# Moving product copies and normal-form evictions to ScalarE, and a bias load by one slot, in an encoder-decoder kernel

## The chip, the cores and the metric

The kernel runs on one core of a Trainium2 chip. Time is the device time of one execution in microseconds, the lower the better. Everything is in fp32. A core has TensorE (PE in the profile, with its weight loads as PEld), VectorE (DVE), ScalarE (ACT), GpSimd (POOL) and SyncE (SP), which here issues every DMA. Each engine has a queue of its own that runs in the order of the program; engines meet at semaphores.

## The reference

One layer of an encoder-decoder with batch 2, width 512, 16 heads of 32, a feed-forward width of 2048, 2048 target rows and 77 source rows. Cut to what matters:

```python
x = src                                    # (2, 77, 512)
x = x + _mha(_ln(x, n1), _ln(x, n1), enc_in, enc_out, enc_bias)
x = x + relu(_ln(x, n2) @ enc_ff1.T + b1) @ enc_ff2.T + b2
memory = x
y = tgt                                    # (2, 2048, 512)
yn = _ln(y, dec_n1)
y = y + _mha(yn, yn, dec_sa_in, dec_sa_out, self_bias + causal)
y = y + _mha(_ln(y, dec_n2), memory, dec_ca_in, dec_ca_out, cross_bias)
h = _ln(y, dec_n3)
y = y + relu(h @ dec_ff1.T + b1) @ dec_ff2.T + b2
```

`_ln` subtracts the mean, divides by the standard deviation, scales and adds. `_mha` projects to q, k and v, takes softmax(q k / sqrt(32) + bias) v for each head and projects out. The biases depend on the difference of positions alone.

## The kernel before

The 2 x 2048 target rows are eight blocks of 512 (two batches of four), each of four tiles of 128 tokens. The instruction order is written out by hand: the program text is the order on every engine.

The attention stage, up to about 1780 us of the span, makes causal self attention of all blocks, with the encoder and the cross attention of the first block (`first_cross`, 960 to 1250 us) in between. After it comes the feed-forward stage, which this change is mostly about. In it each block has 56 slots of feed-forward work, and one generator, `cross(x + 1)`, does the next block's cross attention beside it: before slot n of block x, the generator runs the functions that `plan[n]` holds. `cross(1)` runs ahead of the loop, partly beside the end of self attention; the last block has no companion. Only the fifth block (the first of the second batch) loads a bias in `cross`, for its tiles 0 and 1 (`biased`); those of the first block are loaded in `first_cross`.

The feed-forward matrices are multiplied with seven products instead of eight (`PARTS`): a slot forms one product of sums of quarters. Slots 0 to 27 are the first layer (seven products by four column groups n), slots 28 to 55 the second. `prepare(s + 3)` forms the operands of a slot three slots ahead: on GpSimd, and for the hidden rows of the second layer on VectorE (L1104). `first_product` writes one PSUM bank by eight matmuls (L1121). The bank is used for one or two quarters of the hidden rows `hT`; the first product that reaches a quarter copies into it (L1132, L1134, L1136), later ones add (L1138, VectorE), and after the last one ScalarE applies the relu (L1141). The banks 4 to 7 go round in turn. In the order (1, 4, 5, 7, 2, 3, 6) of all blocks but the first, L1134 runs in slots 0 to 11, once a slot: the second quarter of product 1, of product 4 and of product 5. In the first block's order (3, 5, 1, 4, 7, 2, 6) it runs in slots 0 to 3 and 12 to 15.

`norm_stages` makes a layer norm of a tile in three functions. `stats` has L718 to L720 on VectorE and a power on GpSimd (L721). `center` has L727 on VectorE, which writes the normalized tile into a ring of three buffers, and L728 on GpSimd, which adds a row to y in place. `turned` transposes four 128 x 128 pieces into one PSUM bank on TensorE (L733) and evicts each with scale and bias. In `cross`, the n2 norm of tile t has these in slots t, t + 2 and t + 4, and its results feed the q matmuls (`q_group`, L746) of slots 9 to 12; the n3 norm, which feeds the next block's feed-forward, has `turned` in slots 31, 38, 45 and 52. The y rows are loaded by L998, those of tiles 2 and 3 only after the results that lie in the same place have been stored (L1165) at the end of a block.

`attend_stages` of tile t stand in slots 14 + 7t and after: `score` (matmuls L760, then VectorE: with a bias L767, and L769, L770), `exp` (ScalarE, L773), `normalize` (L778, L779 on VectorE, L780 on GpSimd), `turned` (transposes L786, copies L788 and L790) six slots on, `times_v` (L797, the copy L801) and `out` (L806, L807). The probabilities lie in one buffer, `pr` (named oT in the profile), which the bias tile is loaded into (`bias_tile`, four DMAs, L103) before the scores are added.

Of the kernel before, what the change touches and what calls it, by code (L numbers as in the profile page):

```python
# [11 lines left out]
AF = mybir.ActivationFunctionType  # L12
ALU = mybir.AluOpType
# [4 lines left out]
P = 128  # L18
# [36 lines left out]
def tile_encoder_decoder(ctx: ExitStack, tc: tile.TileContext, ins, out):  # L55
    nc = tc.nc
# [20 lines left out]
    def vec(name, i):  # L77
        c = _COL[name] + i
        return vecs[:, c : c + 1]
# [16 lines left out]
    def bias_tile(dst, m, nq, nk, off):  # L96

        flat = tz[m].rearrange("h b t -> h (b t)")
        for r0 in range(0, nq, RB):
            n = min(RB, nq - r0)  # L100
            o = off - r0
            skew = flat[:, o : o + RB * (LT - 1)].rearrange("h (b u) -> b h u", u=LT - 1)
            nc.sync.dma_start(dst[r0 : r0 + n], skew[:n, :, :nk])  # L103
# [45 lines left out]
    with (  # L149
# [20 lines left out]
        def bank():  # L170

            i = count["bank"] % count["banks"]
            count["bank"] += 1
            return psum[:, i, :]
# [212 lines left out]
        got = {}  # L387
# [322 lines left out]
        def norm_stages(y, n, row, place, done):  # L710

            keep = {}

            def stats():
                st = sm.tile([P, 6], F32, name="bnst", tag="bnst")
                mv = sm.tile([P, 2], F32, name="cmv", tag="cmv", bufs=4)
                rs = sm.tile([P, 2], F32, name="crs", tag="crs", bufs=4)
                nc.vector.bn_stats(st, y())  # L718
                nc.vector.bn_aggr(mv, st)
                nc.vector.tensor_scalar_add(rs[:, 0:1], mv[:, 1:2], EPS)  # L720
                nc.gpsimd.tensor_tensor(rs[:, 1:2], rs[:, 0:1], mhalf[:, 0:1], ALU.pow)  # L721
                keep.update(mv=mv, rs=rs)

            def center():
                xn = keep["xn"] = place()
                mv, rs = keep["mv"], keep["rs"]
                nc.vector.tensor_scalar(xn, y(), mv[:, 0:1], rs[:, 1:2], ALU.subtract, ALU.mult)  # L727
                nc.gpsimd.tensor_tensor(y(), y(), row, ALU.add)  # L728

            def turned():  # L730
                xn, pt, dst = keep["xn"], bank(), done()
                for c in range(NC):
                    nc.tensor.transpose(pt[:, ts(c, P)], xn[:, ts(c, P)], ident)  # L733
                for c in range(NC):
                    sc, bi = vec(f"dec_{n}_s", c), vec(f"dec_{n}_b", c)
                    if c % 2:
                        nc.scalar.activation(dst[:, c, :], pt[:, ts(c, P)], AF.Identity, bias=bi, scale=sc)
                    else:
                        nc.vector.tensor_scalar(dst[:, c, :], pt[:, ts(c, P)], sc, bi, ALU.mult, ALU.add)

            return stats, center, turned

        def q_group(o, w, nT, dst):
            mm = bank()
            for c in range(NC):
                nc.tensor.matmul(mm, w[:, c, :], nT[:, c, :], start=(c == 0), stop=(c == NC - 1))  # L746
            nc.vector.tensor_scalar(dst, mm, vec("dec_ca_in_b", o), SCALE, ALU.add, ALU.mult)
# [140 lines left out]
        for x, (b, m) in enumerate(blocks):  # L888
# [14 lines left out]
            for t in range(TB):  # L903
                end = x == len(blocks) - 1
                jobs[u + NU + (2 if end else 7) + t].append(out_job(b, m, t))
                at = u + NU + ((-1, 0, 3, 4)[t] if end else 6 + t)
# [6 lines left out]
            for g in range(NC):  # L913
# [3 lines left out]
                at = u + g * TB - 3  # L917
# [74 lines left out]
        def y_of(x, t):  # L992
            return ys[x % 2][:, t, :]
# [27 lines left out]
        def late_loads():  # L1021
# [17 lines left out]
        PARTS = {  # L1039

            1: (((1, 1), "+", (2, 2)), ((1, 1), "+", (2, 2)), (("+", 1, 1), ("+", 2, 2))),
            2: (((2, 1), "+", (2, 2)), ((1, 1),), (("+", 2, 1), ("-", 2, 2))),
            3: (((1, 1),), ((1, 2), "-", (2, 2)), (("+", 1, 2), ("+", 2, 2))),
            4: (((2, 2),), ((2, 1), "-", (1, 1)), (("+", 1, 1), ("+", 2, 1))),
            5: (((1, 1), "+", (1, 2)), ((2, 2),), (("-", 1, 1), ("+", 1, 2))),
            6: (((2, 1), "-", (1, 1)), ((1, 1), "+", (1, 2)), (("+", 2, 2),)),
            7: (((1, 2), "-", (2, 2)), ((2, 1), "+", (2, 2)), (("+", 1, 1),)),
# [3 lines left out]
        def order_of(x, layer):  # L1051

            return ORDER[layer if x else 2]
# [20 lines left out]
        def in_ring(name, ring):  # L1074
            turns[name] += 1
            return ring[turns[name] % len(ring)]
# [38 lines left out]
        def first_product(s):  # L1115
            x, layer, i, n = slots[s]
            a, b = operands[s]
            mm = ff_bank()
            for f in range(2):
                for c in range(2):  # L1120
                    nc.tensor.matmul(  # L1121
                        mm[:, ts(f, TOK)], a[:, c, ts(f, P)], b[:, c, :], start=(c == 0), stop=(c == 1)
                    )
            order = order_of(x, 1)
            got = mm.rearrange("p (f n) -> p f n", f=2)
            for k, (sign, r, c) in enumerate(PARTS[i][2]):
                users = [j for j in order if (r, c) in [u[1:] for u in PARTS[j][2]]]
                f = (r - 1) * (NF // 2) + 2 * n
                dst = hT[:, f : f + 2, ts(c - 1, TOK)]
                if i == users[0]:  # L1130
                    if sign == "-":
                        nc.scalar.activation(dst, got, AF.Identity, scale=-1.0)  # L1132
                    elif k:
                        nc.vector.tensor_copy(dst, got)  # L1134
                    else:
                        nc.scalar.copy(dst, got)  # L1136
                else:
                    nc.vector.tensor_tensor(dst, dst, got, SIGN[sign])  # L1138
                if i == users[-1]:
                    for e in range(2):  # L1140
                        nc.scalar.activation(dst[:, e, :], dst[:, e, :], AF.Relu, bias=vec("dec_ff1_b", f + e))  # L1141
# [27 lines left out]
        def ff_bank():  # L1169
            count["mm"] += 1  # L1170
            return psum[:, 4 + count["mm"] % 4, :]
# [11 lines left out]
        def cross(x):  # L1183

            b, m = blocks[x]
            plan = [[] for _ in range(per)]

            def place(tag):
                if tag == "xr":
                    return lambda: sb.tile([P, D], F32, name=tag, tag=tag, bufs=2)  # L1190
                return lambda: in_ring("xt", xt_ring)

            def bias(t):
                bias_tile(pr.rearrange("p (h k) -> p h k", k=S), 2, P, S, 255 - P * t)

            for t in range(TB):
                fs = norm_stages(
                    lambda t=t: y_of(x, t), "n2", bv, place("xt"), lambda t=t: nT2[:, :, ts(t, P)]
                )
                for k, f in zip((0, 2, 4), fs):  # L1200
                    plan[t + k].append(f)
            for g in range(NC):
                plan[9 + g].append(lambda g=g: q_group(g, w_q[g], nT2, qT[g // 2][:, g % 2, :]))
            for t in range(TB):
                at = 14 + 7 * t
                y = lambda t=t: y_of(x, t)
                biased = m == 0 and t < 2
                if biased:
                    plan[at if t else at - 4].append(lambda t=t: bias(t))
                fs = attend_stages(  # L1210
                    lambda g, t=t: qT[g // 2][:, g % 2, ts(t, P)], kTcs[b], vcs[b], y, biased, pr,
                    lambda g: pts_all[:S, g, :], place("xr"), wbt,
                )
                for k, f in zip((0, 2, 3, 6, 9, 11), fs):
                    plan[at + k].append(f)
                fs = norm_stages(y, "n3", bo, place("xt"), lambda t=t: nTt[:, :, ts(t, P)])
                for k, f in zip((13, 15, 17), fs):
                    plan[at + k].append(f)
            for fs in plan:
                for f in fs:  # L1220
                    f()
                yield
# [6 lines left out]
        turned_to, scored_to, at = {n: 0 for n in range(end)}, {}, [0]  # L1229
# [18 lines left out]
        i = 0  # L1248
# [34 lines left out]
        nc.sync.dma_start(w_2, ins["dec_ff2_wT"].rearrange("(c p) o -> p c o", p=P))  # L1283
        count.update(bank=0, banks=4)
        side = cross(1)
        slot(end)
        for s in range(4):
# [12 lines left out]
        for x in range(len(blocks)):  # L1300
            if x:
                side = cross(x + 1) if x + 1 < len(blocks) else iter(())
            for n in range(per):
                if x or n >= 8:
                    next(side, None)
                    ff_slot(x * per + n)
# [37 lines left out]
```

## Time and profile before

| what | value |
|---|---|
| three runs | 2956.04, 2958.81, 2960.45 us (median 2958.81) |
| profiled execution | 2958.76 us, its span 2957.0 us |
| granted TensorE clock, mean over the span | 0.987 |
| L1134, copy on VectorE, 92 times | 684 ns (median) |
| L1136, copy on ScalarE, 32 times | 587 ns (median) |
| L739, eviction on VectorE, 128 times | 409 or 410 ns (medians) |
| L737, eviction on ScalarE, 128 times | 458 ns (median) |
| one block of the feed-forward stage with its companion | about 147 us |

The span is the time from the first to the last instruction on the engines; what lies around it is 1.8 us. In a line of the timeline stand the start, the duration, the engine, the line of the program, the operation, what it writes and reads, and in brackets how long the engine had been idle before and what ended that. In a list of waits stand who waited for whom, the total, the number of times and the longest. The profile puts a wait for several semaphores down to the one that came last.

### The profile page before, as it was taken

How to read it: one execution, taken by the hardware profiler on the slowest of the kernel's cores; microseconds unless marked ns; L12 is line 12 of the kernel's file. 1: busy time of each engine (PE TensorE's matmuls, PEld its weight loads, DVE VectorE, ACT ScalarE, POOL GpSimd, SP SyncE). 2: the span in 40 equal slices, each digit the busy share in tenths (PEclk: the TensorE clock that was granted, in tenths of full speed). 3: DMA queues.
4: the chain of work that ended last, by engine and by line, in shares of the span. 5: the costliest groups of instructions: out<-in, count | busy, mean ns of one | idle time of the engine just before them, and what ended most of it. 6: DMA issues, size and time to landing. Idle time of an engine off the chain costs nothing.

```text
span 2957.0 us, 60689 instructions
## 1 busy us (share of the span) xinstructions
PE 2875.8 (97%) x24440; PEld 2018.7 (68%) x24440; DVE 2202.4 (74%) x6171; ACT 1220.9 (41%) x2211; POOL 737.2 (25%) x601
## 2 busy tenths in 40 slices
PE   8899999999999999999999997999999999999999
PEld 5456666666666556666666675777777777777788
DVE  4767688888987788888878884767676777776765
ACT  3344456546665455555556671213131313131311
POOL 0100000000000101000000004464646464646464
PEclk9799999999999999999999999999999999999999
DMA  6313301201112502201101124000001000000000
GB/s 175 87 52 118 102 16 51 66 16 44 34 41 69 129 19 79 70 26 62 41 16 37 45 75 156 1 29 1 29 1 37 10 29 1 29 1 29 1 15 15
DMA packets 117643, 137.10 MB, mean 46 GB/s; under 512 B 18240, under 2 KB 73072, under 8 KB 117234
## 3 DMA queue, kind: packets, MB, share of 16 engines
q1 hardware_dynamic: 117362, 133.22, 15.5%
q8 instruction: 192, 3.15, 0.5%
q14 instruction: 89, 0.73, 0.1%
HBM read 111.33 MB, written 21.86 MB: 45 GB/s over the span
## 4 chain that ended last, share of the span: by engine, by line
PE 79%; DVE 13%; DMA 3%; issue 2%; POOL 2%; ACT 2%; SPq 0%; POOLq 0%; DVEq 0%; ACTq 0%
PE psum L1152 13%; PE psum L403 12%; PE psum L353 9%; PE psum L1121 8%; PE psum L420 7%; DVE pp L362 5%; PE psum L230 4%; PE psum L806 4%; PE psum L746 4%; PE psum L206 4%; PE psum L242 4%; PE psum L217 3%; DVE pp L369 3%; PE psum L786 2%; PE psum L797 1%
## 5 line engine op out<-in xcount | busy, mean ns | idle before, releaser
L379 ACT ACTIVATE pp<-pp,nm 128x128 f32<-128x128 f32 (+15 forms) x512 | 614.6, 1210 | 200.8 <-DVE nm L376 198.2
L362 DVE TENSOR_SCALAR_CACHE_REDUCE pp<-psum 128x512 f32<-128x512 f32 (+3 forms) x1024 | 558.3, 590 | 47.2 <-PE psum L353 45.3
L403 PE MATMUL psum<-ident,pp 128*128 128x128 f32 x4352 | 549.6, 279 | 18.3 <-DVE mx L369 11.8
L403 PEld LDWEIGHTS psum<-ident,pp 128*128 128x128 f32 x4352 | 475.1, 142 | 132.3 <-DVE pp L362 57.1
L409 ACT COPY pts<-psum 128x512 f32<-128x512 f32 (+3 forms) x592 | 299.1, 577 | 509.6 <-PE psum L403 400.6
L1104 POOL TENSOR_TENSOR vv<-pp 128x512 f32<-128x512 f32 x320 | 415.6, 1316 | 137.4 <-PE psum L1121 117.7
L407 DVE COPY pts<-psum 128x512 f32<-128x512 f32 (+2 forms) x544 | 329.9, 660 | 42.1 <-PE psum L403 39.3
L353 PE MATMUL psum<-kT,q 32*128 32x512 f32 (+3 forms) x2560 | 352.1, 579 | 4.6 <-ACT kT L222 1.6
L420 PEld LDWEIGHTS psum<-pts,vv 128*32 128x32 f32 x8704 | 226.2, 110 | 124.1 <-issue 116.9
L420 PE MATMUL psum<-pts,vv 128*32 128x128 f32 x8704 | 278.7, 275 | 0.2 <-DVE vv L233 0.2
L268 POOL TENSOR_TENSOR rstd<-rstd,mhalf 128x1 f32<-128x1 f32 x32 | 18.2, 570 | 929.8 <-DVE rstd L267 924.4
L1138 DVE TENSOR_TENSOR kT<-kT,psum 128x512 f32<-128x512 f32 x256 | 166.5, 680 | 98.3 <-PE psum L1121 80.5
L1141 ACT ACTIVATE kT<-kT,vecs 128x256 f32<-128x256 f32 x256 | 115.6, 502 | 299.8 <-DVE kT L1138 299.8
L369 DVE CUSTOM_DVE_ANT_0 pp<-psum,bias 128x256 f32<-128x256 f32 (+1 forms) x512 | 209.8, 410 | 20.9 <-PE psum L353 16.6
L353 PEld LDWEIGHTS psum<-kT,q 32*128 32x128 f32 x2560 | 119.4, 184 | 148.6 <-issue 99.4
L1152 PE MATMUL psum<-vv 128*128 128x256 f32 x768 | 176.9, 381 | 0.0
L1121 PE MATMUL psum<-oT,vv 128*128 128x256 f32 x736 | 166.5, 380 | 0.0
L1152 PEld LDWEIGHTS psum<-vv 128*128 128x128 f32 x768 | 143.1, 190 | 26.8 <-issue 9.5
L1121 PEld LDWEIGHTS psum<-oT,vv 128*128 128x128 f32 x736 | 138.8, 190 | 24.4 <-issue 6.2
L1104 DVE TENSOR_TENSOR vv<-kT 128x512 f32<-128x512 f32 x160 | 138.9, 886 | 10.8 <-PE psum L1152 9.9
L253 POOL TENSOR_TENSOR xr<-xr,row_dec_sa_out_b 128x512 f32<-128x512 f32 x32 | 40.7, 1272 | 402.4 <-DMA xr<-in_x_dram 206.3
L1121 PE MATMUL psum<-nT,vv 128*128 128x256 f32 x512 | 119.2, 385 | 16.8 <-POOL vv L1104 15.5
(176 smaller groups left out, 3930.9 us busy)
## 6 DMA issues: line engine op xcount, KB each, us to landing
wqk<-in_dec_sa_in_wT_dram SPq DMA_DIRECT2D x64, 256.0 KB, 3.6
bias<-tz SPq DMA_DIRECT2D x128, 128.0 KB, 3.7
wbig<-in_dec_sa_in_wT_dram SPq DMA_DIRECT2D x8, 1024.0 KB, 7.5
vv<-in_enc_ff_wT_dram SPq DMA_DIRECT2D x8, 1024.0 KB, 5.2
wbig<-in_dec_sa_out_wT_dram SPq DMA_DIRECT2D x8, 1024.0 KB, 7.1
xr<-in_x_dram SPq DMA_DIRECT2D x32, 256.0 KB, 4.5
y<-xr SPq DMA_DIRECT2D x32, 256.0 KB, 2.8
vv<-y SPq DMA_DIRECT2D x32, 256.0 KB, 3.4
```

Source lines behind the costliest of these rows:

```text
L353: nc.tensor.matmul(banks[r][:, : kn * P], q[rows4(r), ts(t, P)], kT[rows4(r), g, k0 * P : (k0 + kn) * P], start=True, stop=True,)
L362: nc.vector.tensor_scalar(p[:, k0 * P : (k0 + far) * P], s[:, : far * P], 1.0, None, ALU.mult, ALU.max, accum_out=st["mx"][:, r, c : c + 1],)
L369: nc.vector.tensor_tensor_reduce(p[:, (i + 1) * P - w : (i + 1) * P], s[:, far * P : kn * P], biases[b, m, g][:, r, 2 * P - w :], 1.0, LOW ...
L379: nc.scalar.activation(p, p, AF.Exp, bias=nm, accum_out=to)
L403: nc.tensor.transpose(pt[:, ts(x, P)], state[n]["p"][r][:, ts(k, P)], ident)
L407: nc.vector.tensor_copy(pts[:, : len(load), :], pt[:, :w])
L409: nc.scalar.copy(pts[:, : len(load), :], pt[:, :w])
L420: nc.tensor.matmul(ot[rows4(r), t, :], vv[:, k, ts(g * HC + r, HD)], got.pop((n, k, r)), start=(k == 0), stop=(k == i),)
L1104: engine.tensor_tensor(dst, quarter(*parts[0], n), quarter(*parts[2], n), SIGN[parts[1]])
L1121: nc.tensor.matmul(mm[:, ts(f, TOK)], a[:, c, ts(f, P)], b[:, c, :], start=(c == 0), stop=(c == 1))
L1138: nc.vector.tensor_tensor(dst, dst, got, SIGN[sign])
L1152: nc.tensor.matmul(mm[:, t, :], lhs[:, c, ts(t, P)], rhs[:, c, :], start=(n == 0 and c == 0), stop=(n == 3 and c == 1),)
```

## The change

Three edits. In `turned` of `norm_stages`, all four evictions of a tile are made by ScalarE; before, VectorE made the first and third. This holds for every use of `norm_stages`: 64 tiles, so 128 evictions move. In `first_product`, every copy of a first use without a minus is made by ScalarE; before, VectorE made it where the quarter was the product's second. 92 copies move. In `cross`, the bias of tile 1 is loaded by the functions of slot 20 instead of slot 21; it is appended to slot 20 behind `turned` of tile 0.

```diff
                 for c in range(NC):
                     sc, bi = vec(f"dec_{n}_s", c), vec(f"dec_{n}_b", c)
-                    if c % 2:
-                        nc.scalar.activation(dst[:, c, :], pt[:, ts(c, P)], AF.Identity, bias=bi, scale=sc)
-                    else:
-                        nc.vector.tensor_scalar(dst[:, c, :], pt[:, ts(c, P)], sc, bi, ALU.mult, ALU.add)
+                    nc.scalar.activation(dst[:, c, :], pt[:, ts(c, P)], AF.Identity, bias=bi, scale=sc)
...
-            for k, (sign, r, c) in enumerate(PARTS[i][2]):
+            for sign, r, c in PARTS[i][2]:
...
                 if i == users[0]:
                     if sign == "-":
                         nc.scalar.activation(dst, got, AF.Identity, scale=-1.0)
-                    elif k:
-                        nc.vector.tensor_copy(dst, got)
                     else:
                         nc.scalar.copy(dst, got)
...
                 if biased:
-                    plan[at if t else at - 4].append(lambda t=t: bias(t))
+                    plan[at - 1 if t else at - 4].append(lambda t=t: bias(t))
```

## The prediction

> **What bounds the kernel.** I read the page's busy shares and slices first, then the last stage by windows, then TensorE's waits there, then the timeline of one block.
>
> ```profile
> PE 2875.8 (97%) x24440; PEld 2018.7 (68%) x24440; DVE 2202.4 (74%) x6171; ACT 1220.9 (41%) x2211; POOL 737.2 (25%) x601
> ...
> PE   8899999999999999999999997999999999999999
> ...
> ACT  3344456546665455555556671213131313131311
> ```
>
> TensorE is busy in 97% of the span, and 81 us are all that any change of other engines can take. In the feed-forward stage, from about slice 24 on, ScalarE is nearly idle; the moved work goes there. Between 1850 and 2957 us the windows give TensorE 1082.8 us busy of 1107, so the stage with nearly all of the edit holds 24 us of idle time. Who ends it:
>
> ```profile
> PE psum L1121 <- POOL vv L1104: 15.5, 1, 15.5
> PE psum L786 <- POOL oT L780: 7.7, 7, 3.2
> PE psum L733 <- ACT vv L737: 3.7, 6, 0.6
> PE psum L806 <- ACT xr L801: 2.9, 1, 2.9
> PE psum L733 <- DVE xt L727: 2.1, 4, 0.6
> PE psum L733 <- DVE pts L727: 2.1, 2, 1.6
> ```
>
> This is TensorE's wait list from 1780 us (total, times, longest). The 15.5 stands before 1806 us and is a load of x; the edit does not touch it. The three L733 rows are what it can reach: 12 waits, two in each of the last six normal-form phases, 7.9 us. One such phase (a block begins at 2413.10; its slots 4 to 7 turn the four token tiles):
>
> ```profile
> 2423.10 0.40 DVE L739 TENSOR_SCALAR vv<-psum,vecs 128x128 f32<-128x128 f32 x1
> 2423.54 0.46 ACT L737 ACTIVATE vv<-psum,vecs 128x128 f32<-128x128 f32 x1 [2.75 <-DVE vv L739]
> 2424.03 0.41 DVE L739 TENSOR_SCALAR vv<-psum,vecs 128x128 f32<-128x128 f32 x1 [0.53 <-ACT vv L737]
> 2424.36 0.54 DVE L727 TENSOR_SCALAR xt<-vv,cmv,crs 128x512 f32<-128x512 f32 x1
> ...
> 2424.95 0.66 PE L733 MATMUL psum<-ident,xt 128*128 128x128 f32 x4 [0.45 <-DVE xt L727]
> ...
> 2427.27 0.54 DVE L727 TENSOR_SCALAR pts<-vv,cmv,crs 128x512 f32<-128x512 f32 x1
> ...
> 2427.95 0.63 PE L733 MATMUL psum<-ident,pts 128*128 128x128 f32 x4 [0.61 <-ACT vv L737]
> ```
>
> The four evictions of a tile go hand to hand between VectorE and ScalarE, 0.94 us from one to the next on the same engine, and VectorE stands 0.53 us in between. Behind them in its queue is L727, which centers the next tile but one, and TensorE waits for that. The 0.61 is put down to L737, which ended at 2427.85, but L727 ended at 2427.81, so either could be the releaser; both hang on the same hand-over.
>
> **The 92 copies (L1134).** 12 in each of seven blocks, 8 in the first. They leave VectorE, 684 ns each in their row, and become L1136, 587 ns. Those that matter are the four in slots 0 to 3, ahead of L727: there VectorE runs late (the copy of slot 3 starts at 2422.51, when TensorE finished that slot at about 2420). Nobody waits for the copies themselves: their line has no waiter, the rows are read again only ten slots later, and a bank comes back after four slots.
>
> **The 128 evictions (L739).** 64 tiles of two: 16 in the attention stage, 56 in the n2 phases, 56 in n3. VectorE loses 0.41 each and the 0.53 between them, so L727 moves up by about 1.3 us a tile. ScalarE gets four in a row after the transposes. No row shows four in a row. [...] Nearest row: L1141's pairs last 0.91 at 497 ns each, a step of 0.41. I take 0.41; a tile then costs 3 x 0.41 + 0.46 = 1.7 us.
>
> [...] Row by row: evictions 458 against 409 ns, so 128 x 0.049 = 6.3 us more; copies 587 against 684, so 92 x 0.097 = 8.9 us less. [...] I go by the rows: ScalarE has the room.
>
> **The block with both edits.** VectorE: stats of tiles 0 and 1 end by 2416.1 instead of 2417.3, tile 0 is centered by about 2417.2. Then the next limit shows: the stats of tile 2 start at 2419.43 today and cannot come sooner, because the load of y (L998, issued 2416.10, 3.4 us to landing) lands at 2419.4. From there 1.0 (stats 2), 0.54 (center 1), 1.0 (stats 3), then center 2, done by 2422.7 even if it waits for a GpSimd operation as the 1.51 us instance of L727 did. TensorE without stalls wants tile 2 at 2424.34 (slots of 1.73 + 0.44 = 2.17 us from 2420.01). Center 3 follows one L1138 later, by 2424.4 against 2426.5. Both waits go. GpSimd's L1104 for slot 8, which comes 0.13 us late today behind L728 (the product starts at 2430.45, the one before ended at 2428.42 + 1.89), goes with them.
> ScalarE: each of slots 4 to 7 costs it 1.7 + 0.5 = 2.2 us; a copy waits for L1138 of its slot, and the next tile's evictions are queued behind it. Starting at 2421.3, tile 3 is done at about 2429.7. Who waits for that is the first q matmul of slot 9 at 2430.45: 0.7 us of cover. If it were gone, that matmul would stall by the excess.
>
> Sum: 7.9 us of L733 waits, and six times 0.13 = 0.8. Taken off: 0.2, because in the block from 2255.3 the second load of y comes late (the stats of tile 3 wait 0.80 us for the DMA and start at 2264.43; 1.0 + 0.54 later, 2266.1, is just when TensorE wants tile 2); and 0.15 in the first block, where four copies fall in slots 12 to 15, two of them now ahead of the exp (L773) in ScalarE's queue: it starts at about 1861.0 instead of 1859.36, and L778 behind it at 1862.3 instead of 1862.16, which the transposes L786 (already 0.38 late) feel. Gain 8.3 us.
>
> **What costs nothing.** n3's 56 evictions: none of the 12 waits lies there, ScalarE has no relu in the second layer. The last block's 12 copies: TensorE runs through it without a wait. The 16 in the attention stage: ends +7.3 us (16 x 0.458, all on the path) and -6.6 (16 x 0.41 of VectorE freed); I take 0, since TensorE is busy 323.5 of 330 us there and ScalarE's L737 now starts sooner (it waited 17.5 us for L739 there).
>
> **The bias load.** It is issued once (cross attention of the fifth block), slot 21 to slot 20: four DMAs, moved on SP's queue past nothing, since slot 20 issues no other.
>
> ```profile
> 2313.28 2.57 PE L786 MATMUL psum<-ident,oT 128*77 128x128 f32 x16 [3.22 <-POOL oT L780]
> ...
> 2315.91 1.90 SPq L103 DMA_DIRECT2D oT<-tz  x4
> ...
> 2321.89 0.48 DVE L767 TENSOR_TENSOR oT<-psum,oT 128x308 f32<-128x308 f32 x1 [1.92 <-PE psum L1121]
> ...
> 2330.89 5.40 PE L806 MATMUL psum<-wbig,xr 128*128 128x512 f32 x8 [2.87 <-ACT xr L801]
> ```
>
> It writes the tile that slot 20's transposes read. They end at 2315.85, SP issues at 2315.91, and one semaphore wait of SP there lasted 50.7 us. The program's order is not what holds it, and in the plan it still stands behind those transposes. Its price stays: VectorE waits until the last bytes land (1.92 us, the releaser named is not the true one), L801 comes late, TensorE stalls 2.87 us and runs L806 in 5.40 us instead of 3.60. I take 0; if it did help, the end is 2.87 + 1.80 = 4.7 us.
> That 1.80 is half clock. [...] The row shows the price after a 2.87 us stall, and the L733 after 0.6 us took 0.63 to 0.66 instead of 0.60, so the short stalls cost only themselves. [...]
>
> **Forecast.** The profiled execution is 2958.76 us (span 2957.0 and 1.8 around it), the median of the runs 2958.81. 2958.76 - 8.3 = 2950.5 us. What a measurement can tell from no change is 0.2%, 5.9 us: faster means below 2952.9.
>
> **Rivals.**
> *The loads of y hold the phase.* VectorE is free and waits for L998; if stats 2 and 3 or the GpSimd power between them come 2 us later than I have it, about half of the stalls stays: 2954.6. For it: stats 2 starts within 0.1 us of the landing today. Against: 1.6 us of room for tile 2, 2.1 for tile 3. 16%.
> *The bias load does come sooner*: 2950.5 - 4.7 = 2945.8. Against: issue 0.06 us after the transposes' end. 5%.
> *ScalarE becomes the bound* in slots 4 to 7 (the other side). With a step p a slot costs it 3p + 0.96; tile 3's first eviction ends at 2421.3 + 3(3p + 0.96) + 0.46. The q matmul waits from p = 0.65 on, and the gain of 1.4 a block is lost from p = 0.80. At 0.94 the stall is 2.65 us, 1.25 x 6 = 7.5 us slower, and with half clock after such stalls up to 1.8 more in each: 2966 to 2977, I put 2970. For it: 0.94 is the only step that these instructions show. Against: that step is two engines', and L1141 shows 0.41. 8%.
> *The attention stage gives the gain back*, ScalarE being 50% busy there: 2957. 8%.
> The forecast has 63%, own range 2948 to 2953.
>
> **Numbers.** Faster: 0.93 x 63 + 5 + a little of the first rival = 66%; slower 8%; the rest, 26%, within 0.2%. The range 2945.5 to 2957.5 leaves out the slower rival, and some 10% beyond it.
>
> **What will show it.** No L733 waits after 1960 us; L737 in fours with a step near 0.41; stats 2 with DMA as its releaser and some us of idle before it; L103 still within 0.1 us of L786's end, and the 1.92, 2.87 and 5.40 unchanged; q matmuls L746 with no ScalarE releaser. L746 waiting for L737, or L403 waiting more in the attention stage, would make it wrong.

## The result, and the profile after

The changed kernel takes 2942.6 us (median of 6 runs, 2939.59 to 2948.41), the kernel before 2958.68 beside it (6 runs, 2952.82 to 2960.45): a ratio of 0.9952, 95% interval 0.9939 to 0.9965. That is 16.1 us faster, where 8.3 were forecast, and below the range. The profiled execution took 2940.9 us with a span of 2939.1, so its span is 17.9 us shorter.

Lines in the changed file have numbers that are one to five lower: L1121 became L1118, L1104 L1101, L1134 and L1136 L1131, L1138 L1133, L739 and L737 L736, L746 L743, L786 L783, L780 L777, L801 L798, L806 L803, L767 L764. The numbers here are those of the kernel that is spoken of.

The busy shares of the changed kernel, and ScalarE in the 40 slices:

```profile
PE 2866.0 (98%) x24440; PEld 2016.6 (69%) x24440; DVE 2101.2 (71%) x5951; ACT 1304.1 (44%) x2431; POOL 742.9 (25%) x601
...
ACT  3344456556666446555556673223232323232321
```

The 220 moved instructions took 101 us from VectorE and gave ScalarE 83. ScalarE's two digits in the feed-forward stage went from 1 and 3 to 2 and 3: it still has room. What TensorE waits for there (changed kernel, list of waits from 1780 us on):

```profile
PE psum L1118 <- POOL vv L1101: 15.0, 1, 15.0
PE psum L783 <- POOL oT L777: 7.6, 7, 3.2
PE psum L803 <- ACT xr L798: 3.7, 1, 3.7
PE psum L1118 <- DVE kT L1133: 0.5, 1, 0.5
```

The three L733 rows, 7.9 us, are gone; the other waits stayed, and the one for L798 grew from 2.9 to 3.7 us. The normal-form phase whose instants the prediction quotes now lies 12 us earlier (timeline of the changed kernel, VectorE, TensorE and ScalarE):

```profile
2407.40 0.69 DVE L718 BATCH_NORM_STATS2 bnst<-vv 128x6 f32<-128x512 f32 x1 [2.30 <-DMA vv<-y]
...
2407.95 0.60 PE L733 MATMUL psum<-ident,pts 128*128 128x128 f32 x4
...
2409.12 1.52 ACT L736 ACTIVATE vv<-psum,vecs 128x128 f32<-128x128 f32 x4
...
2409.88 1.00 DVE L727 TENSOR_SCALAR xt<-vv,cmv,crs 128x512 f32<-128x512 f32 x1
...
2412.29 0.60 PE L733 MATMUL psum<-ident,xt 128*128 128x128 f32 x4
...
2415.93 1.51 ACT L736 ACTIVATE vv<-psum,vecs 128x128 f32<-128x128 f32 x4
...
2418.34 1.88 PE L743 MATMUL psum<-vv,wqk 128*128 128x512 f32 x4
```

VectorE now stands idle for 2.30 us until y has landed. Tile 2 is centered at 2410.88, 1.4 us before TensorE turns it at 2412.29. Four evictions in a row take 1.52 us, a step of (1.52 - 0.46) / 3 = 0.35. The last ones end at 2417.44, 0.9 us ahead of the q matmul.

From the first transpose to that q matmul it is 2418.34 - 2407.95 = 10.39 us. Before, TensorE went through the same stretch like this (timeline of the kernel before):

```profile
2420.01 0.60 PE L733 MATMUL psum<-ident,pts 128*128 128x128 f32 x4
2420.44 1.89 PE L1121 MATMUL psum<-oT,pp 128*128 128x256 f32 x8
2422.17 0.60 PE L733 MATMUL psum<-ident,xt 128*128 128x128 f32 x4
2422.61 1.89 PE L1121 MATMUL psum<-oT,pp 128*128 128x256 f32 x8
2424.95 0.66 PE L733 MATMUL psum<-ident,xt 128*128 128x128 f32 x4 [0.45 <-DVE xt L727]
2425.45 1.89 PE L1121 MATMUL psum<-oT,pp 128*128 128x256 f32 x8
2427.95 0.63 PE L733 MATMUL psum<-ident,pts 128*128 128x128 f32 x4 [0.61 <-ACT vv L737]
2428.42 1.89 PE L1121 MATMUL psum<-oT,pp 128*128 128x256 f32 x8
2430.45 1.99 PE L1121 MATMUL psum<-nT,vv 128*128 128x256 f32 x8
2432.28 2.31 PE L746 MATMUL psum<-vv,wqk 128*128 128x512 f32 x5
```

12.27 us: the phase gave 1.88, where its waits and the late product sum to 0.45 + 0.61 + 0.13 = 1.19. Where nothing holds TensorE, the second L733 starts 1.73 us after the L1121 ahead of it, though that row lasts 1.89: the rows overlap. Why more came than stood in the list is the main question below.

Where the 17.9 us came from, taken start to start of the same TensorE instruction in both traces:

| stretch | gain, us |
|---|---|
| six n2 phases (1.96, 1.98, 3.02, 1.88, 2.02, 1.91) | 12.8 |
| evictions in `first_cross` (966.9 to 992.0, now 23.2 us) | 1.9 |
| half clock at 1523 us, in the profile of before alone | 2.2 |
| half clock at 1057 us, longer in the profile of after | -1.5 |
| the fifth block's cross attention, slots 20 to 25: half clock before, none after | 2.3 |
| start to 967 us, the load of x, small rest | 0.2 |

The first two rows, 14.7 us, lie within the interval of the gain (10 to 18 us). Half clock means that the profile grants TensorE 0.5 of its clock; these rows belong to single executions and are taken up at the end.

### The profile page after: what moved, and what is told of

It is laid out like the page before. It is cut to its first block, busy times and chain, and to the rows that moved or that the text cites. A ratio compares the mean times of both kernels' runs of the same rounds, so it can differ in the third digit from the quotient of the medians.

```text
span 2939.1 us, 60770 instructions
## 1 busy us (share of the span) xinstructions
PE 2866.0 (98%) x24440; PEld 2016.6 (69%) x24440; DVE 2101.2 (71%) x5951; ACT 1304.1 (44%) x2431; POOL 742.9 (25%) x601
## 4 chain that ended last, share of the span: by engine, by line
PE 83%; DVE 12%; ACT 1%; DMA 1%; issue 1%; POOL 1%; SPq 0%; DVEq 0%; POOLq 0%; ACTq 0%
PE psum L1147 13%; PE psum L403 12%; PE psum L1118 10%; PE psum L353 10%; PE psum L420 7%; DVE pp L362 5%; PE psum L206 4%; PE psum L230 4%; PE psum L803 4%; PE psum L743 4%; PE psum L242 4%; PE psum L217 3%; DVE pp L369 3%; PE psum L783 2%; PE psum L757 1%
## 5 line engine op out<-in xcount | busy, mean ns | idle before, releaser
L403 PE MATMUL psum<-ident,pp 128*128 128x128 f32 x4352 | 547.0, 278 | 17.9 <-DVE mx L369 11.8
L1101 POOL TENSOR_TENSOR vv<-pp 128x512 f32<-128x512 f32 x320 | 421.7, 1334 | 145.6 <-PE psum L1118 125.9
L1133 DVE TENSOR_TENSOR kT<-kT,psum 128x512 f32<-128x512 f32 x256 | 166.5, 681 | 136.3 <-PE psum L1118 112.2
L1136 ACT ACTIVATE kT<-kT,vecs 128x256 f32<-128x256 f32 x256 | 115.2, 499 | 185.1 <-DVE kT L1133 185.1
L1118 PE MATMUL psum<-oT,vv 128*128 128x256 f32 x736 | 166.5, 380 | 0.0
L1131 ACT COPY kT<-psum 128x512 f32<-128x512 f32 x124 | 69.6, 588 | 205.6 <-DVE kT L1133 135.0
L1118 PEld LDWEIGHTS psum<-oT,vv 128*128 128x128 f32 x736 | 138.8, 190 | 24.4 <-issue 6.2
L1101 DVE TENSOR_TENSOR vv<-kT 128x512 f32<-128x512 f32 x160 | 133.2, 847 | 15.5 <-PE psum L1147 15.5
```

The source lines that it names most:

```text
L403: nc.tensor.transpose(pt[:, ts(x, P)], state[n]["p"][r][:, ts(k, P)], ident)
L1101: engine.tensor_tensor(dst, quarter(*parts[0], n), quarter(*parts[2], n), SIGN[parts[1]])
L1118: nc.tensor.matmul(mm[:, ts(f, TOK)], a[:, c, ts(f, P)], b[:, c, :], start=(c == 0), stop=(c == 1))
```

## The experiments

Theory A: TensorE was paced by the normal-form phases, VectorE was late in them for want of time, and a stall costs more than its gap in the list. Rivals: the hand-over between two engines on one bank costs by itself; L727 merely stands in the wrong place in VectorE's queue; the extra gain comes from the bias load, from n3 or from ScalarE's copies; or it is chance. Every ratio is against the kernel before on the same chip.

### e1: the evictions alone

```diff
-                    if c % 2:
-                        nc.scalar.activation(dst[:, c, :], pt[:, ts(c, P)], AF.Identity, bias=bi, scale=sc)
-                    else:
-                        nc.vector.tensor_scalar(dst[:, c, :], pt[:, ts(c, P)], sc, bi, ALU.mult, ALU.add)
+                    nc.scalar.activation(dst[:, c, :], pt[:, ts(c, P)], AF.Identity, bias=bi, scale=sc)
```

> Only the 128 evictions moved. Theory A (in the n2 phases TensorE stalls because VectorE is late with L727; any sufficient relief of VectorE there removes all stalls, and each stall costs its gap plus the 0.17 us by which a modelled matmul end lies behind the start of the next): no L733 waits after 1960 us, 2.0 us in each of six phases, and the 1.7 us of the attention stage (974 to 991 us): 2945 us. Theory B (each edit gives its own share and the shares add; here VectorE keeps about half of what leaves it): L733 waits about halved, 2951 us.

2941.54 us, ratio 0.9944 (0.9931 to 0.9958). The six phases gave 12.3 us and `first_cross` 1.87. One L733 wait of 0.3 us is left, in the phase of the fifth block's cross attention, which gave 2.52 instead of 3.02; VectorE waits 0.92 us for a load of y just ahead of it in this profile. The evictions alone bring all but half a microsecond.

### e2: the copies alone

```diff
-                    elif k:
-                        nc.vector.tensor_copy(dst, got)
```

> Only the 92 copies moved. Theory A: center 2 is done by about 0.5 us and center 3 by about 0.3 us before TensorE wants them, so the L733 waits go too, the product of slot 8 stays up to 0.1 late; nothing in the attention stage: 10 to 12 us, 2947.5 us. Theory B: L733 waits about halved: 2952.5 us. A and B differ in the sum: by A the two runs alone gain 13.7 and 11, more than the 16 of both edits together.

2949.52 us, ratio 0.9964 (0.9953 to 0.9975): between the two expectations. The phases gave 8.9 us, `first_cross` nothing; of the 7.9 us of L733 waits 1.1 are left, 0.9 of them in the fifth block's phase, behind 1.40 us in which VectorE waits for a load of y. Together e1 and e2 gain 17.1 + 9.2 = 26.3 us (in the phases 12.3 + 8.9), more than both edits in one kernel (16.1, and 12.8 in the phases): they buy the same thing, time on VectorE ahead of L727. That speaks for A.

### e3: the bias load alone

```diff
-                    plan[at if t else at - 4].append(lambda t=t: bias(t))
+                    plan[at - 1 if t else at - 4].append(lambda t=t: bias(t))
```

> Only the bias load one slot earlier. Theory A: it was held by the transposes, not by the program: the load issues within 0.1 us of the last transpose as before, VectorE's wait for it and the stall of L806 stay: 2958.7 us. Rival (the load comes sooner): 2954 us.

2959.1 us, ratio 1.0004 (0.9993 to 1.0014), 12 runs. The timeline of e3 in the fifth block:

```profile
2313.40 2.49 PE L786 MATMUL psum<-ident,oT 128*77 128x128 f32 x16 [3.21 <-POOL oT L780]
...
2315.97 1.90 SPq L103 DMA_DIRECT2D oT<-tz  x4
...
2330.92 2.12 PE L806 MATMUL psum<-wbig,xr 128*128 128x512 f32 x3 [2.76 <-ACT xr L801]
```

The issue stands 0.08 us after the end of the transposes (0.06 before); the later stall is still there. This edit gives nothing that twelve runs can tell.

### e4: the kernel before, `center` ahead of what shares its slot

```diff
-                    plan[t + k].append(f)
+                    plan[t + k].insert(0 if k == 2 else len(plan[t + k]), f)
```

> Before, with center of tile t + 2 queued ahead of the evictions of tile t on VectorE, nothing moved to another engine. Theory A': only the place of L727 behind the hand-over matters: all L733 waits go, 2947 us. Theory A (VectorE lacks time in slots 0 to 8): the wait of tile 2 goes, that of tile 3 stays at 0.3 us or more, and what is late next is the q matmul of slot 9, by up to 1.3 us: 2953 to 2959 us.

2957.32 us, ratio 0.9994 (0.9985 to 1.0003). TensorE's waits in e4, list from 1780 us on:

```profile
PE psum L746 <- DVE vv L739: 4.5, 6, 0.8
...
PE psum L733 <- DVE pts L727: 0.9, 2, 0.5
PE psum L733 <- DVE xt L727: 0.6, 1, 0.6
```

With L727 moved ahead, most L733 waits go (1.5 of 7.9 us are left), and VectorE is late at the evictions instead: the q matmul waits for L739 in each of the six blocks. Start to start the six phases gave 1.9 us together. The place in the queue is not the cause; VectorE had too much to do between slot 0 and slot 9.

### e5: all four evictions on VectorE

```diff
-                    if c % 2:
-                        nc.scalar.activation(dst[:, c, :], pt[:, ts(c, P)], AF.Identity, bias=bi, scale=sc)
-                    else:
-                        nc.vector.tensor_scalar(dst[:, c, :], pt[:, ts(c, P)], sc, bi, ALU.mult, ALU.add)
+                    nc.vector.tensor_scalar(dst[:, c, :], pt[:, ts(c, P)], sc, bi, ALU.mult, ALU.add)
```

> Before, with all four evictions of a tile on VectorE: no hand-over between the engines, but VectorE has four evictions instead of two and a wait. Theory A (what counts is how long VectorE is held before it reaches L727): four in a row hold it some 1.3 to 1.5 us against 1.26 today, so the L733 waits stay or grow a little: 2958 to 2962 us. Rival (the hand-over from engine to engine is itself what costs, whichever engine does the work): the waits go as in the change, 2946 us.

2957.51 us, ratio 1.0001 (0.9993 to 1.001). The timeline of e5 in the same phase:

```profile
2420.02 1.36 DVE L736 TENSOR_SCALAR vv<-psum,vecs 128x128 f32<-128x128 f32 x4
2421.29 0.54 DVE L727 TENSOR_SCALAR xt<-vv,cmv,crs 128x512 f32<-128x512 f32 x1
...
2421.89 0.66 PE L733 MATMUL psum<-ident,xt 128*128 128x128 f32 x4 [0.43 <-DVE xt L727]
```

There is no hand-over here, and the wait is as long as before (0.43 against 0.45). In the whole list 6.1 of the 7.9 us are left; most of the rest stood in the fifth block's phase, where VectorE waited 0.80 us for a load of y in the profile of before and does not wait in this one. Four evictions hold VectorE from 2420.02 until L727 can start at 2421.29, 1.27 us; hand to hand they held it 1.26 (2423.10 to 2424.36). What frees the path is not fewer hand-overs but VectorE's 1.26 us per tile.

### e6: evictions on ScalarE for the n2 norm in `cross` alone

```diff
-        def norm_stages(y, n, row, place, done):
+        def norm_stages(y, n, row, place, done, act=False):
...
-                    if c % 2:
+                    if c % 2 or act:
...
-                    lambda t=t: y_of(x, t), "n2", bv, place("xt"), lambda t=t: nT2[:, :, ts(t, P)]
+                    lambda t=t: y_of(x, t), "n2", bv, place("xt"), lambda t=t: nT2[:, :, ts(t, P)], True
```

> Before, with the evictions moved to ScalarE only in the n2 norm of the feed-forward stage (56 of 128). Theory A: all of the six phases' gain (12.3 us) and nothing of the attention stage's 1.9: 2946 us. Rival (the 56 evictions of n3 give a part too, by freeing VectorE in the second layer): 2949 us or more.

2946.56 us, ratio 0.9962 (0.995 to 0.9975), as expected. The phases gave 1.90, 1.98, 2.63, 1.88, 2.02 and 1.91, together 12.3, and the whole span is 12.2 us shorter (2944.8). n3's evictions bring nothing. The 1.9 us of `first_cross` appears where its evictions move (e1, the changed kernel, e9) and is zero where they don't (e2, e6).

### e7: the changed kernel, with tile 1's bias loaded into a place of its own

Tile 1's bias is loaded from slot 13 on into a free stretch of `vflat` (`own`), and the add of L767 reads it there (`bt_r` is `own` for this tile and `pr` for the others).

```diff
+        own = vflat[:, 12 * D : 12 * D + H * S]
...
-                        nc.vector.tensor_tensor(d, s, d, ALU.add)
+                        nc.vector.tensor_tensor(d, s, bt_r[:, :, r, :], ALU.add)
...
-                bias_tile(pr.rearrange("p (h k) -> p h k", k=S), 2, P, S, 255 - P * t)
+                bias_tile((own if t else pr).rearrange("p (h k) -> p h k", k=S), 2, P, S, 255 - P * t)
...
-                    plan[at - 1 if t else at - 4].append(lambda t=t: bias(t))
+                    plan[at - 8 if t else at - 4].append(lambda t=t: bias(t))
```

> The changed kernel, with tile 1's bias loaded from slot 13 on into a place of its own (the normal form's, free from slot 13 to 25) instead of the probabilities' buffer. Theory (the load is held by the transposes that read the buffer, and VectorE's wait for it is what delays L798 and stalls L803 by 3.73 us): the wait of 2.99 us goes, the stall goes with it, 3.9 us less than the changed kernel and up to 1.8 more where a stretch of half clock followed it: 2938 us. Rival (L798 is late for another reason): 2942.6 us.

2941.93 us, ratio 0.9948 (0.9934 to 0.9961). The fifth block of the changed kernel, then of e7 (timelines):

```profile
2303.53 1.97 PE L783 MATMUL psum<-ident,oT 128*77 128x128 f32 x16 [3.22 <-POOL oT L777]
...
2311.54 0.48 DVE L764 TENSOR_TENSOR oT<-psum,oT 128x308 f32<-128x308 f32 x1 [2.99 <-DMA oT<-tz]
...
2320.54 3.70 PE L803 MATMUL psum<-wbig,xr 128*128 128x512 f32 x8 [3.73 <-ACT xr L798]
```

```profile
2306.16 3.70 PE L784 MATMUL psum<-ident,oT 128*77 128x128 f32 x16 [3.22 <-POOL oT L778]
...
2314.09 0.47 DVE L765 TENSOR_TENSOR oT<-psum,vv 128x308 f32<-128x308 f32 x1
...
2323.09 3.70 PE L804 MATMUL psum<-wbig,xr 128*128 128x512 f32 x8 [0.86 <-ACT xr L799]
```

The mechanism is as expected: no wait for the DMA, and the stall of 3.73 us is 0.86. The time is not: against the changed kernel's 2942.6 in the first comparison it is 0.7 us better, where 3.9 were expected. In this profile the transposes after the same 3.22 us stall take 3.70 us instead of 1.97, and the granted clock from 2290 to 2330 us is 0.91, against 1.00 in the changed kernel's profile. That is some 7 us at 0.5 (0.09 x 40 / 0.5), by estimate worth up to 3.6 us, more than the 2.9 that the stall gave back. The other four runs have no profile; the mean granted clock of all five is 0.9868, that of the changed kernel's eleven 0.9875, so half clock may have taken part of the gain there too, which is not shown.

### e8: e7, with exp and normalize one slot earlier

```diff
-                for k, f in zip((0, 2, 3, 6, 9, 11), fs):
+                for k, f in zip((0, 1, 2, 6, 9, 11), fs):
```

> e7_own_bias with exp and normalize of each tile one slot earlier in the plan (slots at + 1 and at + 2 instead of at + 2 and at + 3). Theory (the transposes of slot 20 wait 0.81 us in every block for GpSimd's normalization, which hangs on exp standing behind relus in ScalarE's queue and L775 behind L1133 in VectorE's): six waits of 0.81 + 0.17 go, and some 2 of the 3.22 in the fifth block: 7 to 8 us less than e7_own_bias, 2930 us. Rival (L1133, now later, holds up TensorE's banks): 2938 us or more.

2965.18 us, ratio 1.0022 (1.0013 to 1.0031): slower than before, the largest miss. The timeline of e8, GpSimd and TensorE in two blocks:

```profile
2467.24 2.25 POOL L778 TENSOR_TENSOR oT<-oT,cri 128x1232 f32<-128x1232 f32 x1 [4.93 <-DVE cri L777]
...
2469.45 1.27 POOL L1103 TENSOR_TENSOR vv<-pp 128x512 f32<-128x512 f32 x1
...
2470.78 3.54 PE L1120 MATMUL psum<-nT,vv 128*128 128x256 f32 x8 [2.98 <-POOL vv L1103]
...
2769.71 1.99 PE L1120 MATMUL psum<-nT,vv 128*128 128x256 f32 x8 [2.98 <-POOL vv L1103]
```

The stage moved as a whole, with its 2.25 us multiplication on GpSimd, which now stands ahead of L1103. L1103 forms a later slot's operands, and all TensorE work waits for it: seven waits, 22.9 us. The seven waits of the transposes did go, as expected; what was put ahead of L1103 cost more.

### e9: the changed kernel again

No edit.

> The changed kernel once more, for a second profile. Theory (the stretches of half clock fall differently from execution to execution with the same stalls): L733 without waits, L783's 0.81 and 3.22 as in the first profile, start-to-start gains of the six phases again 1.9 to 3.0 us each, but other stretches of half clock behind the stalls of the fifth block than the first profile's none; 2942.6 us within 2.

2944.99 us, ratio 0.9957 (0.9944 to 0.9971), span 2941.4. The phases gave 1.96, 1.98, 3.02, 1.88, 2.02 and 1.91, and `first_cross` 1.88. The gains by stretch repeat to 0.01 us, so they are not chance. Half clock behind the fifth block's stalls was expected to return here; it did not: the granted clock from 2290 to 2330 us is 1.00, as in the first profile.

### e10: the changed kernel, with `normalize` split

`exp` on ScalarE and VectorE's sums (`sums`) run one slot earlier; GpSimd's multiplication stays where it was, so nothing is put ahead of L1104.

```diff
-            def normalize():
+            def sums():
...
-                ri = sm.tile([P, H], F32, name="cri", tag="cri", bufs=2)
+                ri = keep["ri"] = sm.tile([P, H], F32, name="cri", tag="cri", bufs=2)
...
+            def normalize():
+                ri = keep["ri"]
...
-                for k, f in zip((0, 2, 3, 6, 9, 11), fs):
+                for k, f in zip((0, 1, 2, 3, 6, 9, 11), fs):
```

> The changed kernel with exp at slot + 1 and the sums of normalize (VectorE) at slot + 2, the multiplication on GpSimd left at slot + 3, so that GpSimd's order stays. Theory (e8 lost because GpSimd's multiplication moved ahead of the sums L1103 that the next product needs, while exp and the sums really were late): the six waits of 0.81 + 0.17 before the transposes of slot 20 go, some 1 to 2 of the 3.22 in the fifth block: 2935 us. Rival (exp and the sums ahead of L1133 themselves hold up TensorE): 2942 us or more.

2940.89 us, ratio 0.9941 (0.9928 to 0.9953): 4.1 us below e9's median on the same chip; 2935 was expected, and 2942 or more by the rival. The intervals of the two ratios overlap, but all five runs lie below all five of e9. The short waits of the transposes L786 go in six blocks (0.37 us in the first, 0.81 in the others, of which 0.80 is gained, since they still start just as GpSimd ends), and the long one falls from 3.22 to 2.42. In its profile half clock in the fifth block's cross attention stands against that: the granted clock from 2290 to 2330 us is 0.87, where e9's has 1.00.

### e11: e10 with e7's own place for the bias

Both edits above in one kernel.

> e10_split_normalize with the bias of tile 1 in its own place as in e7_own_bias. Theory: the stall of L803 falls from some 3.7 to below 0.9 us as in e7_own_bias, another 2.9 us off e10_split_normalize, less what half clock adds or takes: 2932 us. Rival: the stall of the fifth block's transposes and its half clock make the two equal.

2936.2 us, ratio 0.9924 (0.9911 to 0.9936): 8.8 us below e9's median on the same chip, with intervals that do not meet, and faster than both kernels. The list of waits of e11:

```profile
PE psum L787 <- POOL oT L781: 2.4, 1, 2.4
PE psum L807 <- ACT xr L802: 1.6, 1, 1.6
```

Seven transposes that waited became one, and 3.7 us became 1.6 (below 0.9 was expected).

## Why the prediction was right in kind and wrong in size

**What bounds the kernel: right in the feed-forward stage.** The waits of L733 were the main reach of the change, all of them went, and the time with them. e4 and e5 show why they stood there: VectorE's time ahead of L727, not the order and not the hand-over. "81 us are all that any change of other engines can take" was wrong as a bound: TensorE's idle time fell from 81.2 to 73.1 us, 8.1, and the other 9.8 of the span's 17.9 us came out of what the profile counts as busy (2875.8 and 2866.0 us), mostly the row ends ahead of stalls and half clock.

**The step that failed: "Sum: 7.9 us of L733 waits, and six times 0.13".** The sum takes a stall to cost the idle time that the list shows. That idle time runs from the modelled end of the last matmul, and the end lies too late: eight L1121 take 1.89 us, each lasts 0.38 in its row, so they start (1.89 - 0.38) / 7 = 0.215 apart, and the next one would have started 0.17 before the end that the row gives. The timeline above shows the same without a sum: 1.73 us from an L1121 to the L733 behind it, and 1.89 for the row. A stall behind such a row costs its gap plus 0.17. The prediction had the right number in its hand: it wanted tile 2 at 2424.34, and the row starts at 2424.95, 0.61 late, where the list says 0.45. Start to start, the phase of 2413 lost 0.62 (gap 0.45), 0.78 (0.61) and 0.30 (0.13), and 0.10 at the matmul behind them: 1.8, and 1.88 by its ends. Eighteen stalls by 0.17 are 3.1 us and six times 0.10 are 0.6: with the 8.7 of gaps 12.4. That "the short stalls cost only themselves" was wrong by a little too: behind an L733 that had waited, the next product starts 0.50 and 0.47 us later instead of 0.44, 0.09 a phase and some 0.5 in all. That makes 12.9, where 12.8 was measured, and 12.2 to 12.3 in e6, which moved the n2 evictions alone. The price holds for a stall that was left over as well: e1's one gap of 0.28 us made its phase 0.50 longer, e6's gap of 0.17 made it 0.38 longer. This term was mis-sized by 4 us.

**The 16 evictions of the attention stage: taken as 0, measured 1.9.** Between its two ends (+7.3 and -6.6) the prediction set nothing, since TensorE is busy there. The list of waits of before in that stretch (960 to 1000 us) had a row that speaks against it:

```profile
DVE pp L739 <- ACT pp L737: 2.1, 4, 0.5
```

Four tiles, 0.53 us of VectorE standing idle in each, 2.1 in all. And VectorE lay on the path there. These are the shares by line in the chain that ended last, for before from 966.9 to 992 us and for the changed kernel from 966 to 992 us:

```profile
by line: DVE pp L369 12.4%; DVE pp L739 8.9%; DVE pp L362 8.7%; ACT pp L379 8.2%; DVE xt L274 7.7%; ACT pp L737 7.4%; DVE nm L376 5.6%; DVE nT L293 5.1%; DVE bnst L264 4.9%; PE psum L403 4.8%; DVE pts L407 4.1%; issue 4.0%; DVE kT L727 3.6%
```

```profile
by line: PE psum L217 17.5%; PE psum L242 14.2%; PE psum L206 13.2%; PE psum L353 11.8%; PE psum L403 9.5%; DVE pp L369 9.1%; DVE pp L362 8.2%; PE psum L420 6.9%; DVE nm L376 3.0%; PE psum L439 1.7%; PE psum L733 1.7%; PE psum L286 1.7%; PE
```

L739 and L737 have 16.3% of it before, 4.1 of 25.1 us. VectorE's lines lead the chain before and TensorE's after: VectorE paced this stretch until the evictions left it. As in the phases it is VectorE's whole time that counts, not the hand-over alone: e5 has no such idle time, and gained 0.3 us here. The prediction read a share of a stage where it could have had the row.

**The next limit, the load of y: right.** Stats 2 waits for the DMA, with 1.4 us of room for tile 2 where 1.6 was worked out. That rival, half of the stalls staying, did not come; what it named shows in e1 and e6 as one gap each, 0.28 and 0.17 us behind a late load.

**ScalarE: right.** The step is 0.35 us where 0.41 was taken. The q matmul had 0.9 us of cover where 0.7 was forecast, and no L743 waits for ScalarE. e1 moves work to the engine that is slower at it (458 against 409 ns) and gains 17 us.

**n3 at nothing: right** (e6). **The last block's copies at nothing: right**, since what the changed kernel had gained by the sixth phase, 17.87 us, is what it had gained at the end. **The bias load at nothing: right** (e3); the place it is loaded into holds it, and with a place of its own (e7) the stall goes.

**Numbers.** "1.92, 2.87 and 5.40 unchanged" failed: in the changed kernel VectorE waits 2.99, the stall is 3.73, and its eight matmuls take 3.70. 2.87 + 5.40 = 8.27 became 7.43, because no half clock followed (granted clock 1.00 from 2290 to 2330 us; before, 0.50 from 2331.57 to 2334.98). The width of the forecast's own range, 2948 to 2953, was the author's estimate and no run shows it; the fifth block's cross attention, with half clock before and none after, gave 2.3 us. With the two terms set right the sum is 12.8 + 1.9 = 14.7 us less, 2944.1, between the medians of the two comparisons (2942.6 and 2944.99). Over all executions that list a clock, half clock weighs the same on both sides: the mean granted clock is 0.9877 in 55 executions of the kernel before and 0.9875 in 11 of the changed kernel, and their mean spans, 2956.2 and 2942.2 us, are 14.0 apart. So the two terms are enough, and the rest of the 16.1 us between the medians is spread between executions.

## What to carry over

Take the price of a TensorE stall from starts, not from the idle time in a list: where the next matmul would have begun, by the pitch of its row, against where it did. When a stage is paced by an engine other than the busiest one, look at that engine's own waits before setting its edits to nothing. Moving a stage of work moves all its instructions: before doing so, name what each queue held behind the old place and what it will hold behind the new one (in e8 a GpSimd multiplication that came along stalled TensorE for 22.9 us; e10 left it behind and gained 4.1).

## What the hardware showed beyond that

Half clock did not follow the length of the stall alone. After the same stall of 2.98 us in e8, L1120 took 3.54 us in the block at 2470 and 1.99 in that at 2769; after 3.22 us the transposes took 1.97 in the changed kernel and 3.70 in e7; after 3.73 us L803 took 3.70 in the changed kernel, and after 2.87 us L806 took 5.40 in before. It also came where TensorE hardly stood still. The windows of before and of e4 from 1515 to 1535 us, where both programs are the same (columns: window, length, busy time and number of instructions of PE, PEld, DVE, ACT and POOL, granted clock, DMA share, GB/s):

```profile
1515.00:1535.00 20.00, 19.67 (x152) 12.10 (x152) 15.06 (x50) 7.80 (x10) 0.00 (x0) 0.83 0.00 1
```

```profile
1515.00:1535.00 20.00, 19.67 (x166) 11.15 (x168) 16.94 (x53) 7.88 (x11) 0.00 (x0) 1.00 0.01 1
```

The granted clock is 0.83 in one and 1.00 in the other, with the same busy time, 19.67 of 20 us, in which 152 instructions ran in one and 166 in the other. From 1000 us on the profile of before has 30.7 us of half clock (a last stretch at the very end of each span left out), that of after 20.5; at half speed those 10.2 us are by estimate worth up to 5.1 us. Start to start they were worth 3.0, the three half clock rows of the table, which is nearly all that the span's 17.9 us has over the 14.7 of the two terms.

In the profile of before these stretches at 0.50 are 3.41, 6.83, 13.65, 3.41 and 3.41 us long, from 1058.39, 1522.61, 1795.67, 2314.50 and 2331.57 us on; in that of after 6.83 and 13.65, from 1055.79 and 1793.07 us on. In the feed-forward stage the granted clock does not go by the length of the stalls. These are windows with TensorE's stalls in them, to the decimals of the timelines and lists of waits:

| profile | window, us | stalls, us | granted clock |
|---|---|---|---|
| before | 2300 to 2340 | 3.22, 2.87 | 0.91 |
| e4 | 2300 to 2340 | 3.2, 3.7 | 0.96 |
| e6 | 2290 to 2330 | 3.2, 3.3 | 0.91 |
| changed kernel | 2290 to 2330 | 3.22, 3.73 | 1.00 |
| e9 | 2290 to 2330 | 3.2, 3.7 | 1.00 |
| e7 | 2290 to 2330 | 3.22, 0.86 | 0.91 |
| e10 | 2290 to 2330 | 2.4, 3.8 | 0.87 |
| e11 | 2290 to 2330 | 2.4, 1.6 | 1.00 |
| e8 | 2160 to 2175 | 2.98 | 0.89 |
| e8 | 2765 to 2780 | 2.98 | 1.00 |

Stalls of 3.2 and 3.7 us have 1.00 in two profiles and 0.96 in a third, and in e8 2.98 us have 0.89 in one block and 1.00 in another. From 1515 to 1535 us the granted clock is 0.83 in before, e3 and e6, and 1.00 in the changed kernel, e4, e7, e9, e10 and e11. No run set half clock on purpose, and what decides where it comes stays open.
